# First loads of a DiT block: Wada's first half shared with ScalarE's queue, Wqkv's q and k in four pieces, the bias of the modulation added in four parts

## Chip, cores and metric

The kernel runs on one core of one Trainium2 chip. The metric is the device time of one execution in microseconds; several executions are given as a median with the lowest and the highest.

## What is computed

One transformer block with adaptive layer norm, in float32: x is 2 x 2048 x 512, 16 heads of 32, a hidden layer of 2048.

```python
mod = jax.nn.silu(condition) @ Wada + bada          # 2 x 3072
sh_a, sc_a, gt_a, sh_m, sc_m, gt_m = jnp.split(mod, 6, axis=1)
xn = _layernorm(x, g1, be1)
xm = xn * (1.0 + sc_a[:, None, :]) + sh_a[:, None, :]
x = x + gt_a[:, None, :] * _attention(xm, Wqkv, Wproj, bproj)   # causal
xn = _layernorm(x, g2, be2)
xm = xn * (1.0 + sc_m[:, None, :]) + sh_m[:, None, :]
h = jax.nn.gelu(xm @ W1 + b1, approximate=False)
x = x + gt_m[:, None, :] * (h @ W2 + b2)
```

## The kernel before

Batch row 0 is projected first (`Qkv`: four groups of 512 tokens), then its attention runs, then the same for batch row 1 with the output projection of row 0 ahead of it, and at last the two layers of the MLP for all tokens. The change touches only what stands ahead of and inside the first of these stages.

Ahead of the first group the kernel does this. Seven small DMAs on ScalarE's queue (line 1102) bring the condition and the columns of parameters (g1, be1, g2, be2, b1, b2) as rows of one tile, `rows`. SyncE's queue brings the four tiles of x of group 0 (`load_x`, line 796), then parts 0 and 1 of Wada (`load_wada`, line 1120: for each of the four chunks k of 128 rows, one DMA of 256 KB for either part), then Wqkv (`load_w`, line 803: q, k and v, 1 MB each), then the x of group 1. GpSimd brings bada into the tile `mr` (line 1114).

The computation around it, in the order in which each engine has it:

- PE: `ps_c` (line 212, the transpose of `rows`), eight transposes of the first two x tiles (`ps_xt`), the sixteen passes of `ps_mod` (the modulation, silu of the condition times Wada, line 1148), eight transposes of the other two x tiles, `ps_modt` (line 1158: `mr` to columns, four products of two passes each), then group 0's products: `ps_qk` (line 842; q and k blocks of 128 columns in turn) and `ps_v`.
- DVE: the statistics of the four x tiles (line 216), some constants, `cols` (line 1130, a copy of `ps_c`), the reciprocal of the standard deviations (line 223), the four normalized x tiles (line 241), then `mr` (line 1153, `ps_mod` plus bias), the columns a and c, and with ScalarE the modulated tokens `xmT`.
- ScalarE: its DMAs, a table load and a first square root, `rstd` (line 222), another table load, and the silu of the condition (`sc`, line 1184), which needs `cols`.

Nothing of x goes through `ps_mod`; the two meet in `xmT`. Still each engine works in order, and so `ps_xt` stands behind `ps_c`, `ps_mod` behind the first `ps_xt`, and the reciprocal behind `cols`.

The framework that schedules the kernel orders instructions on DVE, ScalarE, GpSimd and the queues by its own estimate; PE's order, and what is wrapped in `act`, is that of the program. It gives the DMAs issued by SyncE and ScalarE eight completion counters, one after the other in turn. A DMA that gets a counter again waits, before it is issued, until the DMA that had that counter eight DMAs earlier has landed. All that the queue holds behind it waits too. In the program before, the DMAs come in this order: cond, x0, g1, x1, be1, g2, x2, be2, x3, b1, b2, the eight of Wada, the three of Wqkv, the four of the next x. So x3 waits for cond, b1 for x0, b2 for g1, the first of Wada for x1.

Later in this stage `load_wada(2, 5)` is called in group 0 and `load_wada(3, 4)` in group 1, all on SyncE's queue; their modulations run in groups 1 and 2, between the products. `columns` adds the bias in each of the three calls; for parts 2 and 5 it then ends, since these are gates that are kept as rows.

Of the kernel before, what the change touches and what calls it, by code (L numbers as in the profile page):

```python
# [12 lines left out]
ALU = mybir.AluOpType  # L13
# [4 lines left out]
P = 128  # L18
# [9 lines left out]
def dit_block_kernel(  # L28
# [36 lines left out]
    nc = tc.nc  # L65
    B, T, D = x.shape
# [17 lines left out]
    def pool(name, bufs=1, **kw):  # L84
        return tc.tile_pool(name=name, bufs=bufs, reuse_waits="tile", **kw)
# [31 lines left out]
    for n in range(2):  # L117

        f = bp.tile([P, QB + P], BF16, tag=f"fold{n}", name=f"fold{n}")
# [10 lines left out]
    def picks():  # L130
        two = ident.rearrange("p (k r b) -> p k r b", k=2, r=2)[:, :, :, :B]
        nc.vector.tensor_tensor(pickc, two[:, 0], two[:, 1], ALU.add)
# [6 lines left out]
    cols = const.tile([P, 64], F32, tag="cols", name="cols")  # L139
# [55 lines left out]
    def col(r, n):  # L195
        return cols[:, r : r + n]
# [5 lines left out]
    def mm(*args, **kw):  # L202

        return tc.keep_in_program_order(nc.tensor.matmul(*args, **kw))  # L204

    def act(ins):

        return tc.keep_in_program_order(ins)

    def transpose(dst, src):  # L210
        n = src.shape[0]
        return tc.keep_in_program_order(nc.tensor.transpose(dst, src, ident[:n, :n]))  # L212
# [571 lines left out]
    class Qkv:  # L784
# [12 lines left out]
                xts.append(xt)  # L797
            self.xts[g] = xts

        def load_w(self, queue):  # L800
            w_v = Wqkv.rearrange("(c p) f -> p c f", p=P)
            for f in range(0, 3 * D, D):
                act(queue.dma_start(self.w[:, :, f : f + D], w_v[:, :, f : f + D]))

        def stats(self, g, t, keep=False):

# [282 lines left out]
    with pool("wada") as wp, pool("qkv0") as qp, pool(  # L1089
        "ps_qkv0", bufs=6, space=PSUM  # L1090
    ) as ps_mm:
        rows = wp.tile([n_rows, P], F32, tag="rows", name="rows")
        for r, n, src in (
            (0, n_cond, cond.rearrange("b (c p) -> (b c) p", p=P)),
            (r_g1, C, g1.rearrange("(c p) -> c p", p=P)),
            (r_be1, C, be1.rearrange("(c p) -> c p", p=P)),
            (r_g2, C, g2.rearrange("(c p) -> c p", p=P)),
            (r_be2, C, be2.rearrange("(c p) -> c p", p=P)),
            (r_b1, FC, b1.rearrange("(c p) -> c p", p=P)),
            (r_b2, C, b2.rearrange("(c p) -> c p", p=P)),  # L1100
        ):
            nc.scalar.dma_start(rows[r : r + n, :], src)
        wada_v = Wada.rearrange("(c p) f -> p c f", p=P)
        wada = {}

        def load_wada(s0, s1):
            w = wp.tile([P, 2, C, D], F32, tag="wada", name="wada")
            if s0 % 3 == 2:
                mr = modr
            else:  # L1110
                mr = wp.tile([P, D], F32, tag="mr", name="mr")
                nc.gpsimd.memset(mr, 0.0)
            for n, s in enumerate((s0, s1)):
                nc.gpsimd.dma_start(
                    mr[n * HD : n * HD + B, :],
                    bada[s * D : (s + 1) * D].partition_broadcast(B),
                )
            for k in range(C):
                for n, s in enumerate((s0, s1)):
                    nc.sync.dma_start(w[:, n, k, :], wada_v[:, k, s * D : (s + 1) * D])  # L1120
            wada[s0] = w, mr

        qkv = Qkv(row, qp, ps_mm)
        qkv.load_x(0)
        load_wada(0, 1)
        qkv.load_w(nc.sync)

        ps_c = ps_mm.tile([P, n_rows], F32, tag="mm", name="ps_c")
        transpose(ps_c, rows)
        nc.vector.tensor_copy(cols[:, :n_rows], ps_c)  # L1130
        sc = wp.tile([P, C, HD], F32, tag="sc", name="sc")
        nc.vector.memset(sc, 0.0)

        def modulation(s0):

            w, mr = wada.pop(s0)  # L1140
            ps = ps_sp.tile([P, D], F32, tag="s", name="ps_mod")
            for k in range(C // 2):
                for half in range(2):
                    for n in range(2):
                        at = (2 * half + n) * HD
                        kk = half * C // 2 + k
                        mm(
                            ps[at : at + HD, :], sc[:, kk, :], w[:, n, kk, :],
                            start=(k == 0), stop=(k == C // 2 - 1),
                        )  # L1150

            def columns():
                nc.vector.tensor_tensor(mr, ps, mr, ALU.add)
                if s0 % 3 == 2:
                    return
                ps_t = ps_sp.tile([P, C, 2, B], F32, tag="s", name="ps_modt")
                for k in range(C):
                    mm(
                        ps_t[:, k], mr[:, k * P : (k + 1) * P], pickc,
                        start=True, stop=True,  # L1160
                    )
                nc.vector.tensor_copy(
                    mod[:, s0 : s0 + 2], ps_t.rearrange("p c s b -> p s c b")
                )

            return columns

        def scale_shift(a, c, r_g, r_be, shift, scale):

            for dst, r in ((a, r_g), (c, r_be)):  # L1170
                nc.vector.scalar_tensor_tensor(
                    dst, mod[:, scale], 1.0,
                    col(r, C).unsqueeze(2).to_broadcast([P, C, B]),
                    ALU.add, ALU.mult,
                )
            nc.vector.tensor_tensor(c, c, mod[:, shift], ALU.add)

        for t in range(MTT):
            qkv.stats(0, t)
        qkv.normalize(0, 0)  # L1180
        halves = [qkv.norm(0, 0)]

        act(
            nc.scalar.activation(
                sc[:, :, :B], col(0, n_cond).rearrange("p (b c) -> p c b", c=C), AF.Silu
            )
        )
        picks()
        columns = modulation(0)
        qkv.normalize(0, 1)  # L1190
        halves.append(qkv.norm(0, 1))
        columns()
        scale_shift(a1, c1, r_g1, r_be1, 0, 1)
        for k in range(0, C, 2):
            for modulate in halves:
                modulate((k, k + 1))
        act(nc.vector.tensor_copy(pick, pickc.unsqueeze(3).to_broadcast([P, 2, B, P])))

        def also(g, n):

            if g == NG - 1 and n % 2 == 0:
                quarters.step()
            if g == 0 and n == 2:
                load_wada(2, 5)
            elif g in (1, 2) and n == 3:
                qkv.columns = modulation(g + 1)
            elif g in (1, 2) and n == 4:
                qkv.columns()
                if g == 1:
                    load_wada(3, 4)  # L1210
                else:
                    scale_shift(a2, c2, r_g2, r_be2, 3, 4)

        quarters = Quarters()
        with pool("hl0") as hp:

            def rooms():

                w = wp.tile([P, 2 * C * D], F32, tag="wada", name="w7")
                return [w[:, k * piece : (k + 1) * piece] for k in range(2)]  # L1220

            quarters.more_rooms = rooms
            qkv.run(hp, also)
            quarters.store()
# [5 lines left out]
    with pool("qkv1") as qp, pool("ps_qkv1", bufs=6, space=PSUM) as ps_mm:  # L1230
        qkv = Qkv(row, qp, ps_mm)
# [725 lines left out]
```

## Time and profile before

| | us |
|---|---|
| median of 3 executions | 2307.09 |
| lowest, highest | 2304.53, 2312.58 |
| the profiled execution | 2305.74 |
| its span, first to last instruction | 2304.0 |
| mean granted TensorE clock | 0.999 |
| PE busy in the span | 2257.0 |

The views used below are the page's busy shares, the busy time by stretches, the instructions in order of time, the waits, and the instructions of one tile. "PE" are TensorE's products, "PEld" its weight loads, "SPq", "ACTq" and "POOLq" the DMA issues of an engine. In the order of time a row gives start, duration, engine, line, operation, output and inputs, the count of merged instructions, and in brackets how long the engine was idle before and what ended that. In a stretch's row stand start and end, length, the busy time and count of each engine, the granted clock, the DMA engines' busy share and GB/s. Packets and sizes of DMAs are decimal in GB/s; a tile of 128 x 512 float32 is 256 KB.

### The profile page before, as it was taken

The numbers are of one execution on the slowest core, as the hardware profiler recorded it, in microseconds if no ns is written. First come the engines' busy times: TensorE is split into PE (matmuls) and PEld (weight loads), VectorE is DVE, ScalarE is ACT, GpSimd is POOL, SyncE is SP. The second block draws the span as 40 slices with busy tenths as digits, with TensorE's granted clock in tenths as the row PEclk, the third lists the DMA queues.
The fourth block names the chain that finished last, engine by engine and source line by source line (L and its number), as shares of the span: only waits on it lengthen the run. The fifth ranks groups of instructions, "written<-read, shape, count | busy, mean of one in ns | idle before, by whom it ended". The sixth has DMA issues, their size and how long they took to land. (4 is left out here: it accounts for less than half of the span.)

```text
span 2304.0 us, 33430 instructions
## 1 busy us (share of the span) xinstructions
PE 2257.0 (98%) x12141; PEld 1385.4 (60%) x12141; DVE 1544.9 (67%) x3089; ACT 940.6 (41%) x1780; POOL 1290.5 (56%) x1036
## 2 busy tenths in 40 slices
PE   8999999999999999999999999999999999999998
PEld 3455555555544445544555545446888888888887
DVE  3367776777766525667677777555896876877787
ACT  2222555555565122245555555632332242252230
POOL 1042987878793564468789787553664602602510
PEclk9999999999999999999999999999999999999999
DMA  7678206151233799971421504265375654654643
GB/s 256 201 224 208 63 24 136 31 120 47 59 130 117 245 303 308 322 231 29 93 69 34 116 24 131 87 226 197 119 272 202 210 177 160 201 181 151 213 145 116
DMA packets 118524, 355.60 MB, mean 154 GB/s; under 512 B 14496, under 2 KB 15052, under 8 KB 103640
## 3 DMA queue, kind: packets, MB, share of 16 engines
q1 hardware_dynamic: 107040, 293.64, 42.4%
q0 software_dynamic: 10944, 59.28, 7.2%
q8 instruction: 96, 1.57, 0.3%
q14 instruction: 68, 0.56, 0.1%
q10 hardware_dynamic: 376, 0.55, 0.1%
HBM read 253.80 MB, written 107.48 MB: 157 GB/s over the span
## 5 line engine op out<-in xcount | busy, mean ns | idle before, releaser
L608 ACT ACTIVATE e<-st 128x512 f32<-128x512 f32 (+1 forms) x1152 | 573.4, 579 | 403.2 <-PE st L204 358.0
L473 DVE TENSOR_REDUCE mx<-s 128x1 f32<-128x512 f32 x612 | 413.4, 687 | 193.3 <-PE s L204 192.0
L638 POOL TENSOR_TENSOR ee<-ee,e 128x1024 f32<-128x1024 f32 x212 | 498.6, 2385 | 7.6 <-ACT e L608 7.6
L204 PE MATMUL s<-kst,qst 128*128 128x512 f32 (+3 forms) x1032 | 472.7, 459 | 11.9 <-DVE mx L473 5.8
L204 PE MATMUL st<-qst,kst 128*128 128x512 f32 (+3 forms) x1280 | 400.9, 378 | 0.0
L204 PE MATMUL ps_a<-sum,room 128*128 128x256 f32 x1504 | 356.8, 381 | 4.7 <-DVE c L1440 1.7
L204 PEld LDWEIGHTS ps_a<-sum,room 128*128 128x128 f32 x1504 | 281.2, 190 | 54.5 <-issue 6.0
L204 PE MATMUL o<-e,vv 128*32 128x512 f32 (+3 forms) x2560 | 303.0, 539 | 5.1 <-POOL e L617 5.1
L468 DVE CUSTOM_DVE_ANT_0 junk<-s,causal 128x128 bf16<-128x128 f32 (+3 forms) x420 | 206.1, 491 | 124.2 <-PE s L204 116.7
L204 PEld LDWEIGHTS s<-kst,qst 128*128 128x128 f32 x1032 | 193.9, 188 | 143.4 <-issue 65.2
L204 PEld LDWEIGHTS st<-qst,kst 128*128 128x128 f32 x1280 | 229.0, 188 | 68.1 <-issue 38.9
L638 POOL TENSOR_TENSOR ee<-e 128x1024 f32<-128x1024 f32 x84 | 198.3, 2381 | 122.5 <-ACT e L608 114.9
L204 PE MATMUL ps_qk<-xmT,wqkv 128*128 128x512 f32 x512 | 239.0, 594 | 1.8 <-DVE xmT L275 1.8
L617 POOL TENSOR_SCALAR_AFFINE_SELECT e<-e 128x256 f32<-128x256 f32 x256 | 103.7, 438 | 94.4 <-ACT e L608 92.3
L204 PEld LDWEIGHTS ps_qk<-xmT,wqkv 128*128 128x128 f32 x512 | 93.9, 190 | 97.2 <-issue 90.5
L1668 POOL TENSOR_TENSOR c<-c,h 128x512 f32<-128x512 f32 x40 | 58.6, 1485 | 159.4 <-ACT c L1666 159.4
L204 PEld LDWEIGHTS <-sel 32*128 32x128 bf16 x1152 | 29.7, 91 | 192.4 <-issue 190.3
L204 PE MATMUL ps_b<-sum,room 128*128 128x256 f32 x608 | 143.6, 379 | 0.0
L204 PEld LDWEIGHTS o<-e,vv 128*32 128x32 f32 x2560 | 61.8, 108 | 104.3 <-issue 80.3
L204 PEld LDWEIGHTS ps_b<-sum,room 128*128 128x128 f32 x608 | 115.0, 190 | 15.4
L204 PE MATMUL ps_v<-wqkv,xmT 128*128 128x512 f32 x256 | 122.1, 594 | 0.0
L204 PE MATMUL st<-fold,sel 32*128 32x512 bf16 (+1 forms) x1152 | 117.6, 372 | 4.3 <-DVE mhl L494 2.8
(180 smaller groups left out, 2939.2 us busy)
## 6 DMA issues: line engine op xcount, KB each, us to landing
qst<-q SPq DMA_DIRECT2D x128, 256.0 KB
room<-w1e SPq DMA_DIRECT2D x28, 1024.0 KB
kst<-k SPq DMA_DIRECT2D x24, 1024.0 KB
room<-w1e SPq DMA_DIRECT2D x28, 768.0 KB
room<-w2e SPq DMA_DIRECT2D x21, 1024.0 KB
q<-hl SPq DMA_DIRECT2D x32, 512.0 KB
k<-hl SPq DMA_DIRECT2D x32, 512.0 KB
room<-w2e SPq DMA_DIRECT2D x21, 768.0 KB
```

Of the source, the lines that this page charges most:

```text
L204: return tc.keep_in_program_order(nc.tensor.matmul(*args, **kw))
L468: nc.vector.tensor_tensor_reduce(junk[:, :w], s[:, :w], causal[:, QB - w :], 1.0, MASKED, ALU.add, ALU.max, m,)
L473: nc.vector.tensor_reduce(m, s[:, :w], axis=AX.X, op=ALU.max)
L608: act(nc.scalar.activation(e[:, h % 2, :w], sts[h][:, :w], AF.Exp))
L617: nc.gpsimd.affine_select(d, d, pattern=[[0, 2], [1, P]], compare_op=ALU.is_ge, fill=0.0, base=0, channel_multiplier=-1,)
L638: act(engine.tensor_tensor(dst, x, y, ALU.add))
L1668: nc.gpsimd.tensor_tensor(c, c, piece_of(base, i, t, pair), ALU.add)
```

## The change

Chunks 0 and 2 of Wada's parts 0 and 1 are issued by ScalarE, chunks 1 and 3 by SyncE, each as one DMA of both parts (512 KB). ScalarE's rows are split: cond stays first, the six others are written in the program behind x and Wada. Wqkv's q and k come in halves of 256 columns, q, k, q, k, and then v whole. The bias is added in four parts of 128 columns, except for parts 2 and 5. `load_wada(3, 4)` has adjoining parts too and becomes four DMAs on SyncE; `load_wada(2, 5)` stays at eight.

```diff
-        def load_w(self, queue):
+        def load_w(self, queue, cols=range(0, 3 * D, D), n=D):
             w_v = Wqkv.rearrange("(c p) f -> p c f", p=P)
-            for f in range(0, 3 * D, D):
-                act(queue.dma_start(self.w[:, :, f : f + D], w_v[:, :, f : f + D]))
+            for f in cols:
+                act(queue.dma_start(self.w[:, :, f : f + n], w_v[:, :, f : f + n]))
...
-        for r, n, src in (
+        rows_of_cols = (
...
-        ):
-            nc.scalar.dma_start(rows[r : r + n, :], src)
+        )
+
+        def load_rows(some):
+            for r, n, src in some:
+                nc.scalar.dma_start(rows[r : r + n, :], src)
...
             for k in range(C):
+                queue = nc.scalar if s0 == 0 and k % 2 == 0 else nc.sync
+                if s1 == s0 + 1:
+                    queue.dma_start(
+                        w[:, :, k, :],
+                        wada_v[:, k, s0 * D : (s1 + 1) * D].rearrange(
+                            "p (n d) -> p n d", d=D
+                        ),
+                    )
+                    continue
                 for n, s in enumerate((s0, s1)):
                     nc.sync.dma_start(w[:, n, k, :], wada_v[:, k, s * D : (s + 1) * D])
             wada[s0] = w, mr
 
         qkv = Qkv(row, qp, ps_mm)
+        load_rows(rows_of_cols[:1])
         qkv.load_x(0)
         load_wada(0, 1)
-        qkv.load_w(nc.sync)
+        load_rows(rows_of_cols[1:])
+        half = D // 2
+        qkv.load_w(nc.sync, (0, D, half, D + half), half)
+        qkv.load_w(nc.sync, (2 * D,))
...
             def columns():
-                nc.vector.tensor_tensor(mr, ps, mr, ALU.add)
+                per = D if s0 % 3 == 2 else P
+                for k in range(0, D, per):
+                    part = mr[:, k : k + per]
+                    nc.vector.tensor_tensor(part, ps[:, k : k + per], part, ALU.add)
```

PE's instructions and their order are the same in both programs.

## The prediction

> **What bounds the kernel now.** I read the busy shares first, then PE by stage, then the first microseconds in order of time.
>
> ```profile
> PE 2257.0 (98%) x12141; PEld 1385.4 (60%) x12141; DVE 1544.9 (67%) x3089; ACT 940.6 (41%) x1780; POOL 1290.5 (56%) x1036
> ...
> 0.00:20.00 20.00, 9.40 (x44) 5.31 (x45) 10.05 (x35) 4.88 (x9) 6.31 (x20) 1.00 0.88 303
> 20.00:160.00 140.00, 139.36 (x419) 67.82 (x418) 62.30 (x167) 36.89 (x63) 21.48 (x30) 1.00 0.72 219
> ```
>
> PE is busy 98% of the span. Of its 47 us of idle time, 10.6 lie in the first 20 us, and only 0.64 in the next 140, in which batch row 0 is projected. The edits lie in those two stretches. So what moves is when the first `ps_qk` starts: from there PE runs without a gap, and what stands behind it in order moves by as much. This is the start in order of time (start, duration, instruction, idle before it and its releaser):
>
> ```profile
> 0.81 2.39 SPq L796 DMA_DIRECT2D x<-in_x_dram  x4
> 3.54 0.69 ACTq L1102 DMA_DIRECT2D rows<-in_L_cond_b_dram  x2
> 3.54 0.69 DVE L216 BATCH_NORM_STATS2 stat<-x 128x6 f32<-128x512 f32 x1 [2.17 <-DMA x<-in_x_dram]
> 4.26 1.28 ACT L136 ACT_TABLE_LOAD   x1 [4.26 <-DMA x<-in_x_dram]
> 4.43 3.81 SPq L1120 DMA_DIRECT2D wada<-in_L_cond_Wada_dram  x8
> 4.43 0.69 DVE L216 BATCH_NORM_STATS2 stat<-x 128x6 f32<-128x512 f32 x1
> 6.84 0.66 DVE L216 BATCH_NORM_STATS2 stat<-x 128x6 f32<-128x512 f32 x1
> 7.23 0.30 PE L212 MATMUL ps_c<-ident,rows 44*128 44x44 f32 x1 [7.23 <-DMA rows<-in_L_cond_b_dram]
> 7.75 0.30 ACT L222 ACTIVATE rstd<-mv,eps 128x4 f32<-128x4 f32 x1 [1.99 <-DVE mv L219]
> 8.00 0.15 DVE L115 COPY tmask<-tmask 128x1 f32<-128x1 f32 x1
> 8.06 0.20 DVE L1130 COPY cols<-ps_c 128x44 f32<-128x44 f32 x1
> 8.24 0.17 DVE L223 RECIPROCAL rstd<-rstd 128x4 f32<-128x4 f32 x1
> 8.28 2.48 SPq L803 DMA_DIRECT2D wqkv<-in_L_cond_Wqkv_dram  x3
> 9.12 2.21 PE L212 MATMUL ps_xt<-ident,x 128*128 128x128 f32 x8 [1.59 <-DVE x L241]
> 11.27 3.86 PE L204 MATMUL ps_mod<-wada,sc 128*32 128x512 f32 x16
> 12.11 0.18 PEld L204 LDWEIGHTS ps_mod<-wada,sc 128*32 128x32 f32 x2 [0.66 <-DMA wada<-in_L_cond_Wada_dram]
> 12.81 0.35 PEld L204 LDWEIGHTS ps_mod<-wada,sc 128*32 128x32 f32 x6 [0.51 <-DMA wada<-in_L_cond_Wada_dram]
> 13.45 0.37 PEld L204 LDWEIGHTS ps_mod<-wada,sc 128*32 128x32 f32 x2 [0.29 <-DMA wada<-in_L_cond_Wada_dram]
> 14.08 0.14 PEld L204 LDWEIGHTS ps_mod<-wada,sc 128*32 128x32 f32 x2 [0.27 <-DMA wada<-in_L_cond_Wada_dram]
> 15.06 0.86 PEld L212 LDWEIGHTS ps_xt<-ident,x 128*128 128x128 f32 x8 [0.84 <-issue]
> 15.22 0.69 DVE L1153 TENSOR_TENSOR mr<-ps_mod,mr 128x512 f32<-128x512 f32 x1 [4.78 <-issue]
> 15.97 0.97 PEld L204 LDWEIGHTS ps_modt<-pickc,mr 128*128 128x128 f32 x8
> 18.80 24.30 PE L204 MATMUL ps_qk<-xmT,wqkv 128*128 128x512 f32 x56 [1.78 <-DVE xmT L275]
> ```
>
> Two things must meet before `ps_mod`: Wada, and a chain from the rows of parameters: `ps_c`, `cols`, on DVE then the reciprocal and the normalized x, `ps_xt`, `ps_mod`. The rows end at 7.23, x at 6.84; Wada's waits then cost 0.66 + 0.51 + 0.29 + 0.27 = 1.73 us inside `ps_mod`, which is what the change can win.
>
> The rows also show how DMAs are issued. The eight completion counters of SyncE's and ScalarE's DMAs are used in turn, and a DMA is not issued before the one eight earlier has landed. ScalarE's b1 stood eight behind the first x and was issued at 3.54, when that landed; SyncE's first Wada stood eight behind the second x and went at 4.43, when that landed. SP's waits say the same:
>
> ```profile
> SPq L1120 <- DMA x<-in_x_dram: 1.5, 2, 1.2
> ```
>
> **Half of Wada on ScalarE: what it moves.** In the built program the DMAs now come in this order: cond, x0, Wada chunk 0 (ACT), x1, x2, Wada chunk 2 (ACT), x3, Wada chunk 1 (SP), g1, be1, g2, Wada chunk 3 (SP), be2, b1, b2, Wqkv. So eight back from g2 is Wada chunk 0, and eight back from b1 is Wada chunk 2: 512 KB pieces. b1 can't be issued before 1 MB of Wada has landed through ScalarE's queue. b2 stands behind it, then ACT's table load (1.28), a column of 0.2 and `rstd` (0.30), which so end at least 2.5 after b1's issue; the rows need longer, as follows. `ps_c` takes all the rows, is first on PE, and `cols` stands ahead of the reciprocal on DVE. The rows, off the critical side before, now end last.
>
> When does chunk 2 land? The first x has the DMA engines to itself; then ScalarE's 4 quarter megabytes share them with SyncE's x1 to x3 and half of chunk 1. If the queues take turns, chunk 2 is the ninth quarter megabyte. Before, the ninth (four x and five of Wada) was there at 12.11: that wait of `ps_mod` is for chunk 2, whose first piece was Wada's fifth. The bounds come from the rates:
>
> ```profile
> 2.00:14.00 12.00, 5.18 (x22) 2.67 (x23) 6.07 (x20) 3.28 (x5) 3.40 (x8) 1.00 0.92 304
> 14.00:22.00 8.00, 6.22 (x31) 3.48 (x27) 3.51 (x10) 1.93 (x4) 1.55 (x3) 1.00 1.05 393
> ```
>
> Nine quarters are 2.36 MB. At 393 GB/s from 2.0 on they end at 8.0; if ScalarE's queue comes last of all Wada, at 14.08. I take 12.1, the row that counts landings of the same pieces. [...]
>
> From b1's issue to `ps_c` it took 7.23 - 3.54 = 3.69 us, with x and Wada under way; the same pair goes out again beside Wada and Wqkv, so I take 3.69. The low bound is the first x on empty queues, 0.81 to 3.54: 2.73. From `ps_c` the reciprocal needs 0.30 + 0.06 (to `cols`) + 0.18 = 0.54; before it was 1.01, since DVE was busy to 8.06 with `tmask`. So the reciprocal comes at 12.1 + 3.69 + 0.54 = 16.33 instead of 8.24: 8.09 late, and with it `ps_xt` and `ps_mod`, which follow as before.
>
> **What is won.** By 19.4 (16.33 and the 3.03 from 8.24 to 11.27) all Wada has landed, so the 1.73 of waits go. Not all of that is gained, for TensorE was slow while they passed:
>
> ```profile
> L212 PE MATMUL ps_xt<-ident,x x8: 421/421/474, 9.1 to 10.9; 128*128 128x128 f32 x8
> L212 PE MATMUL ps_xt<-ident,x x8: 272/272/330, 15.1 to 15.9; 128*128 128x128 f32 x8
> L204 PE MATMUL ps_mod<-wada,sc x16: 592/892/1062, 11.3 to 14.5; 128*32 128x512 f32 x16
> ```
>
> The same transpose takes 421 ns at 9.1 us and 272 at 15.1, a `ps_mod` pass 1062 at first and 592 at last: twice the pace, from somewhere near four microseconds after the first `ps_xt`. `ps_mod`'s 16 passes lie in four column strips side by side, four deep. The fast pace is 24.30 / 56 = 0.43 a pass, the slow one twice that, 0.87. With two slow and two fast passes and 0.16 to drain it takes 2.76 instead of 3.86: 1.10 won. Bounds: all slow 0.2, all waits 1.73. [...]
>
> **Bias in four parts: nothing.** `ps_modt` can't start before the second `ps_xt` block leaves PE, 15.06 + 0.86 = 15.92, and the whole add ends at 15.22 + 0.69 = 15.91. Four adds of 128 columns cost between 0.20 each (`cols`' 44 columns) and 0.69 / 2 = 0.35: they end 0.8 to 1.4 after 15.22, and the last pair of `ps_modt` is only due at 15.97 + 0.73 = 16.70. If they took longer than 1.5, PE would wait for the rest. The later use (parts 3 and 4, in group 2) lies in the stretch where PE idles 0.64 in 140.
>
> **Wqkv in pieces, and SP's queue.** The first piece is issued when Wada chunk 1 has landed, later than 8.28. `ps_qk` would start at 18.80 + 6.99 = 25.8. From 14.1 the q and k pieces (2.1 MB) need 5.3 us at 393 GB/s and 6.9 at 304: they end by 21.0, V by 24.4, the next x by 27.9, for statistics first due at about 34. No row shows rows of 1 KB; were they half as fast as 304, the first two pieces would still be there at 21. Cost nothing either way; without the delay above, pieces in turn would let the first K block start half a megabyte sooner, which nobody waits for (the 1.78 before `ps_qk` is for xmT). Of Wada's parts 2 and 5, four pieces now stand ahead of the first q store on SP and the rest behind it; they are needed a group later. DVE and ACT change their order in group 0 to 2 a little; PE's cover there is the 0.64.
>
> **Sum.** +8.09 - 1.10 = +6.99, on the profiled execution's 2305.74 us (span 2304.0): **2312.7 us**. That run is 1.35 under the median shown, 2307.09, by which it would be 2314.1. A measurement of this kernel tells about 0.3% from no change, 6.9 us here: the forecast sits on that bound.
>
> **Rivals.** *Not slower: chunk 2 lands early.* If ScalarE's pieces get past x or the engines run at 393 from the start, chunk 2 lands at 8.0: 8.0 + 3.69 + 0.54 - 8.24 = 3.99, less 1.10: +2.9, 2308.6. With 2.73 for the rows and all 1.73 won it is +1.3, 2307.0. It decides below a landing of 12.0; for it speaks the mean rate of 304, by which nine quarters end at 9.8, against it that x's four (1.05 MB, 5.5 by that rate) landed only at 6.84. *Later still:* chunk 2 comes with the last of Wada, 14.08: 14.08 + 4.23 - 8.24 - 1.10 = +9.0, 2314.7; with 0.2 won, 2315.6. *The change does what it says:* the rows don't bind, Wada is early: -1.1 to -1.7, 2304.0 to 2304.6; within the bound too. For it: only if counters were not used in turn, which 3.54 and 4.43 contradict.
>
> **How the numbers follow.** Forecast with its own spread (landing 12 to 13.5) 0.42; later still 0.10; chunk 2 before 12.0 0.40; no delay 0.08. Slower by over 0.3%: 0.52. Within: 0.43, the early cases. Faster: 0.05, out of the last case and the runs' own spread (2304.53 to 2312.58), since 6.9 us are not to be had from 1.73. The range goes from the early case's low end, 2306.5, to the late one's high end on the median, 2317.5.
>
> **What would show it.** Right: `ps_c` ends its wait near 15.8 on a b row, ACT's b issues start near 12.1, `ps_mod` has no wait on Wada and takes about 2.8, `ps_qk` starts near 25.8, PE in 20 to 160 stays as full. Wrong: b issued before 9, or `ps_qk` before 20; a PE wait on Wqkv; a shift that is not the same at the start of attention and at the end.

## The result, and the profile after

Over 22 executions of each on the same chip the changed kernel takes 2311.01 us (2304.69 to 2315.15), the kernel before 2306.93 (2302.95 to 2312.78): ratio 1.0016, 95% interval 1.0009 to 1.0023. It is slower, by 3.7 us (0.0016 x 2306.93): within the 0.3% that the prediction called no change, though so many executions tell it apart from none. The medians themselves lie 4.08 apart. The profiled execution took 2309.83 us (span 2308.1), 4.09 more than before's.

The rows that answer to those of before are the busy shares and the stretches first:

```profile
PE 2258.2 (98%) x12141; PEld 1386.3 (60%) x12141; DVE 1547.9 (67%) x3095; ACT 941.0 (41%) x1780; POOL 1294.4 (56%) x1036
...
0.00:20.00 20.00, 6.87 (x30) 3.17 (x31) 7.36 (x29) 3.17 (x5) 4.76 (x17) 1.00 0.88 311
20.00:160.00 140.00, 137.59 (x412) 66.89 (x411) 61.26 (x167) 36.86 (x63) 18.19 (x26) 0.99 0.69 211
2.00:14.00 12.00, 0.87 (x3) 0.48 (x4) 5.48 (x19) 3.17 (x5) 3.40 (x8) 1.00 0.93 333
```

PE has 2.53 us less work in the first 20 us and 1.77 less in the next 140: 4.30 in all, the delay of the first `ps_qk`. The DMA engines moved 333 GB/s from 2 to 14 us where they had moved 304. The gain lies early, from 4 to 10 us (the first row is before's), and ends in a lull:

```profile
4.00:10.00 6.00, 1.18 (x4) 0.78 (x5) 5.16 (x20) 3.28 (x5) 1.40 (x3) 1.00 0.89 279
4.00:10.00 6.00, 0.00 (x0) 0.00 (x0) 3.12 (x10) 0.33 (x1) 1.40 (x3) 1.00 1.06 394
10.00:12.00 2.00, 0.00 (x0) 0.00 (x0) 0.42 (x5) 1.97 (x4) 0.00 (x0) 1.00 0.39 125
```

394 GB/s instead of 279: x and Wada had moved by 11.1, all but a hundredth of them by 10.5, where `ps_mod` had waited for Wada up to 14.08. Wada was thus there sooner, as the change wants; the rows now came last. Then the start of the changed kernel in order of time:

```profile
1.41 0.93 ACTq L1125 DMA_DIRECT2D wada<-in_L_cond_Wada_dram  x2
2.65 2.16 SPq L1125 DMA_DIRECT2D wada<-in_L_cond_Wada_dram  x2
3.60 0.69 DVE L216 BATCH_NORM_STATS2 stat<-x 128x6 f32<-128x512 f32 x1 [2.24 <-DMA x<-in_x_dram]
8.96 0.69 ACTq L1105 DMA_DIRECT2D rows<-in_L_cond_b_dram  x2
9.01 0.69 DVE L216 BATCH_NORM_STATS2 stat<-x 128x6 f32<-128x512 f32 x1 [1.27 <-DMA x<-in_x_dram]
12.09 0.30 PE L212 MATMUL ps_c<-ident,rows 44*128 44x44 f32 x1 [12.09 <-DMA rows<-in_L_cond_b_dram]
12.55 0.17 DVE L223 RECIPROCAL rstd<-rstd 128x4 f32<-128x4 f32 x1
13.43 2.21 PE L212 MATMUL ps_xt<-ident,x 128*128 128x128 f32 x8 [1.03 <-DVE x L241]
15.57 3.64 PE L204 MATMUL ps_mod<-wada,sc 128*32 128x512 f32 x16
19.14 1.37 PE L212 MATMUL ps_xt<-ident,x 128*128 128x128 f32 x8
19.34 0.88 DVE L1173 TENSOR_TENSOR mr<-ps_mod,mr 128x128 f32<-128x128 f32 x4 [4.59 <-issue]
20.36 0.95 PE L204 MATMUL ps_modt<-pickc,mr 128*128 128x4 f32 x8
23.09 5.40 PE L204 MATMUL ps_qk<-xmT,wqkv 128*128 128x512 f32 x8 [1.78 <-DVE xmT L275]
```

The mechanism is the predicted one. b1 and b2 are issued late, at 8.96, `ps_c` waits for them to 12.09, and the reciprocal, `ps_xt` and `ps_mod` follow. The reciprocal is 4.31 late (12.55 against 8.24), and `ps_qk` 4.29 (23.09 against 18.80). `ps_mod` no longer waits for Wada, but its passes all took the long time:

```profile
L204 PE MATMUL ps_mod<-wada,sc x16: 1061/1061/1062, 15.6 to 18.2; 128*32 128x512 f32 x16
```

So only 0.22 of its 3.86 went, not 1.10. And the first passes of `ps_qk` are long too; the granted clock stands third from the end of each stretch's row:

```profile
20.00:22.00 2.00, 1.31 (x13) 1.22 (x11) 0.80 (x6) 0.00 (x0) 0.53 (x1) 1.00 1.01 340
22.00:24.00 2.00, 0.92 (x1) 0.44 (x2) 1.97 (x5) 1.32 (x3) 1.03 (x2) 0.80 0.94 329
24.00:26.00 2.00, 2.00 (x4) 0.93 (x3) 0.27 (x1) 0.61 (x2) 0.00 (x0) 0.50 0.95 333
26.00:28.00 2.00, 2.00 (x5) 0.77 (x5) 0.00 (x0) 0.00 (x0) 0.00 (x0) 0.85 0.29 107
```

Half clock for 0.8 + 2.0 + 0.6 = 3.4 us costs 1.7. In the kernel before, the same stretch of `ps_qk` has a clock of 1.00:

```profile
20.00:22.00 2.00, 2.00 (x6) 0.85 (x5) 0.00 (x0) 0.32 (x1) 0.00 (x0) 1.00 1.05 382
```

Instruction by instruction against before, PE is 4.28 late at the first `ps_qk`, 5.98 after its long passes, and still 5.8 at 400 us. It is 2.4 late at 1001, because before loses 1.3 more in a wait between 980 and 1000 us and 1.7 in a window of half clock there, while the changed kernel has its own only after 1030. At the end it is 4.17. The last figure is thus 4.3 of delay, and windows of half clock that fall here in the one execution and there in the other. Over many executions the windows do not make the difference: the mean granted clock of the changed kernel's 22 is 0.9984, that of the kernel before 0.9984 to 0.9987 in the four groups below. Times 2305 us that is 3.8 us lost against 3.1 to 3.7.

### The profile page after: what moved, and what is told of

It is laid out like the page before. It is cut to its first block, busy times and chain, and to the rows that moved or that the text cites. A ratio compares the mean times of both kernels' runs of the same rounds, so it can differ in the third digit from the quotient of the medians.

```text
span 2308.1 us, 33431 instructions
## 1 busy us (share of the span) xinstructions
PE 2258.2 (98%) x12141; PEld 1386.3 (60%) x12141; DVE 1547.9 (67%) x3095; ACT 941.0 (41%) x1780; POOL 1294.4 (56%) x1036
```

## Experiments

All were run in five rounds beside the kernel before, in four groups on four chips (2305.25, 2304.53, 2305.83 and 2306.59 are the medians of before in them), so that ratios compare across groups and times do not. PE's delay in a profile is that of one execution; the ratio is of the medians.

**The Wada part alone.** The kernel before with only this part of the diff: chunks 0 and 2 on ScalarE's queue, adjoining parts as one DMA, six rows behind them.

```diff
+                queue = nc.scalar if s0 == 0 and k % 2 == 0 else nc.sync
...
+        load_rows(rows_of_cols[:1])
         qkv.load_x(0)
         load_wada(0, 1)
+        load_rows(rows_of_cols[1:])
```

> Before plus Wada's split alone (half of its first chunks on ScalarE, 512 KB each, six of the seven rows behind it); Wqkv stays in three pieces, the bias in one add. Theory: the whole cost is this part, through the counter that b1 shares with Wada's chunk 2: b1 issued near 9, ps_c near 12.1, ps_qk from 23.1, time +2.5 to +5 us on the kernel before. Rival: the pieces of Wqkv or the four adds carry part of it: then less than +2.

2310.45 us against 2305.25, ratio 1.0020 (1.0011 to 1.0029).

```profile
8.99 0.69 ACTq L1105 DMA_DIRECT2D rows<-in_L_cond_b_dram  x2
12.02 0.30 PE L212 MATMUL ps_c<-ident,rows 44*128 44x44 f32 x1 [12.02 <-DMA rows<-in_L_cond_b_dram]
15.50 2.43 PE L204 MATMUL ps_mod<-wada,sc 128*32 128x512 f32 x16
21.64 2.84 PE L204 MATMUL ps_qk<-xmT,wqkv 128*128 128x512 f32 x6 [1.78 <-DVE xmT L275]
```

The b rows, `ps_c` and `ps_mod`'s start are those of the whole change to 0.1 us: this part carries all of the cost in time (1.0020 against the whole change's 1.0016). Here TensorE turned fast inside `ps_mod`, so that 1.43 was won (3.86 - 2.43) and `ps_qk` is 2.84 late. Its profiled execution was the shortest of its eleven, 2305.54; the median is what counts.

**The other two parts alone.** The kernel before with Wqkv in pieces and the bias in four parts.

```diff
-        qkv.load_w(nc.sync)
+        qkv.load_w(nc.sync, (0, D, half, D + half), half)
+        qkv.load_w(nc.sync, (2 * D,))
```

> The other two parts alone: Wqkv's q and k in four pieces and the bias in four adds, Wada as before. Theory: nothing, within 1 us of the kernel before; ps_c at 7.2, ps_modt still not before the second ps_xt block leaves PE, ps_qk at 18.8 plus or minus 0.2, no PE wait on Wqkv. Rival: rows of 1 KB are slow and the next x or Wqkv is late, or four adds end later than ps_modt needs them: +1 to +3 us, with a wait in ps_modt or ps_qk.

2306.76 against 2305.25, ratio 1.0001 (0.9991 to 1.0011): nothing that can be told apart, as predicted. `ps_qk` starts 0.16 later and no instruction of PE waits for Wqkv.

```profile
18.96 5.21 PE L204 MATMUL ps_qk<-xmT,wqkv 128*128 128x512 f32 x8 [1.78 <-DVE xmT L275]
...
20.00:22.00 2.00, 2.00 (x4) 0.96 (x3) 0.14 (x1) 0.48 (x2) 0.00 (x0) 0.50 1.05 384
```

The window of half clock in `ps_qk` is here too, without a late row: it does not come from the late rows.

**All rows first.** The changed kernel, with the seven rows ahead of x and Wada again.

```diff
-        load_rows(rows_of_cols[:1])
+        load_rows(rows_of_cols)
         qkv.load_x(0)
         load_wada(0, 1)
-        load_rows(rows_of_cols[1:])
```

> The changed kernel with all seven rows of parameters issued ahead of x and Wada on ScalarE's queue, so that no row takes over a counter from Wada. Theory (counters): b1 issued near 3.5, ps_c at 7.2 to 7.5; ScalarE's table load waits for the issue of chunk 2 (behind the third x), so rstd some 0.5 later than before; ps_xt near 9.6, ps_qk 18.5 to 19.5, time within 1 us of the kernel before. Rival (sharing): the second queue by itself makes x late, the fourth x at 9.0 instead of 6.8 as in the changed kernel: then ps_xt not before 11, ps_qk from 20.5, time +2 us.

2308.32 against 2305.25, ratio 1.0013 (1.0003 to 1.0023).

```profile
3.56 0.69 ACTq L1105 DMA_DIRECT2D rows<-in_L_cond_b_dram  x2
4.43 1.15 ACTq L1125 DMA_DIRECT2D wada<-in_L_cond_Wada_dram  x2
13.20 0.20 PEld L204 LDWEIGHTS ps_mod<-wada,sc 128*32 128x32 f32 x8 [2.14 <-DMA wada<-in_L_cond_Wada_dram]
19.62 4.56 PE L204 MATMUL ps_qk<-xmT,wqkv 128*128 128x512 f32 x10 [1.78 <-DVE xmT L275]
```

The late rows are cured (b at 3.56, `ps_xt` at 8.73), but now `ps_mod` begins at 10.87 and, after the passes of its first chunk, waits 2.14 for the next, which by its order is chunk 2 of ScalarE's queue, and `ps_qk` is still 0.82 late. Neither theory had this whole. Wada was issued only from 4.2 on, and its next chunk was waited for to 13.20, where the changed kernel had all of Wada by 11.1: the second queue alone does not bring it sooner. The time is another matter: `ps_qk` comes 3.5 us earlier than in the changed kernel, and the ratio falls only from 1.0016 to 1.0013, well inside the intervals. That the late rows make the loss in time is thus read from the changed kernel's profile; this run does not confirm it.

**One queue, in order of use.** The same, and Wada's four 512 KB chunks all on SyncE in the order in which `ps_mod` takes them.

```diff
-            for k in range(C):
-                queue = nc.scalar if s0 == 0 and k % 2 == 0 else nc.sync
+            for k in (0, 2, 1, 3):
+                queue = nc.sync
```

> All seven rows first, and Wada's four chunks of 512 KB all on SyncE's queue in the order in which ps_mod reads them (0, 2, 1, 3); Wqkv in pieces and the bias in four parts stay. Against the run with the rows first, in which chunk 2 came from ScalarE and ps_mod stood 2.14 us for it. Theory (two queues that take turns bring all chunks in at the end, one queue brings them in order): no PE wait over 0.8 on Wada, ps_qk at 18.2 to 19.0, time within 1 us of the kernel before and 1 to 2 less than with the rows first. Rival (512 KB pieces land late on any queue): a wait of 1.5 or more stays.

2305.38 against 2304.53, ratio 1.0004 (0.9995 to 1.0012).

```profile
17.77 10.61 PE L204 MATMUL ps_qk<-xmT,wqkv 128*128 128x512 f32 x17 [1.78 <-DVE xmT L275]
...
18.00:20.00 2.00, 2.00 (x3) 0.94 (x4) 0.95 (x3) 1.29 (x3) 0.00 (x0) 0.50 1.05 384
20.00:22.00 2.00, 2.00 (x3) 0.67 (x2) 0.00 (x0) 0.00 (x0) 0.00 (x0) 0.50 1.07 384
```

`ps_qk` starts 1.03 earlier than before, and 1.85 earlier than with two queues: here the loads do gain. Whether the one queue or the order of use does it was not separated, and the ratio is no clear gain on 1.0013. In the profile two windows of half clock, from 17.1 to 23.9, give back 3.0.

**b1 and b2 issued by GpSimd.** The changed kernel, with only these two rows taken off ScalarE's queue.

```diff
-                nc.scalar.dma_start(rows[r : r + n, :], src)
+                queue = nc.gpsimd if r in (r_b1, r_b2) else nc.scalar
+                queue.dma_start(rows[r : r + n, :], src)
```

> The changed kernel with the b1 and b2 rows issued by GpSimd, whose queue has counters of its own; cond and the other four rows stay on ScalarE behind Wada's two chunks. It splits the delay of the rows: the counter of b1 (nothing is issued before chunk 2 has landed at 9.0) against standing in ScalarE's queue behind 1 MB. Theory (counter): be2 goes out near 7.3 as before, so the rows are complete near 9.5 to 10.3 instead of 12.1, ps_c then; 2 us less than the changed kernel, +1 to +3 on the kernel before. Rival (the queue): rows behind 1 MB of Wada land no sooner than 11.5 to 12, and nothing is won.

2310.28 against 2304.53, ratio 1.0028 (1.0018 to 1.0038).

```profile
7.67 0.26 ACTq L1106 DMA_DIRECT2D rows<-in_L_cond_be_dram  x1
12.38 0.30 PE L212 MATMUL ps_c<-ident,rows 44*128 44x44 f32 x1 [12.38 <-DMA rows<-in_L_cond_be_dram]
```

be2 is issued at 7.67, 1.3 earlier than b1 was, and `ps_c` still waits for it to 12.38: 4.7 us for 2 KB, where the b rows took 3.1 and 3.7 from issue to `ps_c`. The counter of b1 was thus not the only hold (be2 itself follows g2, which goes out only at 7.32). be2 stands in ScalarE's queue behind 1 MB of Wada, and the 12.38 lies near the 11.5 to 12 of the rival that puts the delay there; that its place in the queue is the cause was not isolated. Open too is the time: `ps_qk` starts at 20.66, 2.4 earlier than in the changed kernel, with no window of half clock in this stage, and the median is still 5.75 above before.

**Products ahead of `ps_c`.** The changed kernel, with 36 products of the identity with itself (72 passes) on PE while it waits for the rows. Nobody reads their results.

```diff
+        for _ in range(4):
+            ps_w = ps_mm.tile([P, 512], F32, tag="mm", name="ps_warm")
+            for k in range(9):
+                mm(ps_w[:, :P], ident, ident, start=True, stop=True)
         transpose(ps_c, rows)
```

> The changed kernel with 36 products of the identity (72 passes) ahead of ps_c, whose result nobody reads; they fill PE's idle time while the rows are awaited, to about 11.5. Theory (the pace of TensorE follows its own activity): ps_c still near 12.1, the first ps_xt block in 1.3 or less instead of 2.2, ps_mod in about 1.9 instead of 3.6, ps_qk near 20.3 and no slow passes in it, so 3 to 4.5 us less than the changed kernel: within 1 us of the kernel before. Rival (the slow passes belong to what they read, tiles just landed by DMA): ps_mod keeps 3.6 and the time stays that of the changed kernel.

2303.74 against 2305.25, ratio 0.9994 (0.9984 to 1.0005).

```profile
12.91 1.44 PE L212 MATMUL ps_xt<-ident,x 128*128 128x128 f32 x8 [0.24 <-DVE x L241]
14.63 1.92 PE L204 MATMUL ps_mod<-wada,sc 128*32 128x512 f32 x16 [0.28 <-ACT sc L1208]
20.19 4.10 PE L204 MATMUL ps_qk<-xmT,wqkv 128*128 128x512 f32 x9 [1.82 <-issue]
```

With PE busy beforehand, `ps_mod` takes 1.92, a little over half of 3.64: it is the pace and not Wada that held it. `ps_qk` is 1.36 late instead of 4.29. That is 2.9 better. The rest of the profile's gain (it ends 4.1 ahead of the kernel before) comes between 997 and 1031 us, where this execution has neither a window of half clock nor the 3 us of idle time that before has from 1000 to 1040.

**The same on the kernel before**, with 16 products (32 passes):

```diff
+        for _ in range(2):
+            ps_w = ps_mm.tile([P, 512], F32, tag="mm", name="ps_warm")
+            for k in range(8):
+                mm(ps_w[:, :P], ident, ident, start=True, stop=True)
         transpose(ps_c, rows)
```

> The kernel before with 16 products of the identity (32 passes) on PE ahead of ps_c, to about 7.0. Theory (activity): the first ps_xt block takes 1.5 instead of 2.2, ps_mod's passes are fast, but its end is set by the landing of the last Wada piece near 14, so ps_qk comes 0.2 to 0.6 earlier at most; what else is won is that no execution has slow passes in ps_qk: -0.5 to -2 us in the median. Rival (no slow passes in most executions of the kernel before): within 0.5 us.

2307.0 against 2304.53, ratio 1.0008 (0.9999 to 1.0017): a miss. `ps_mod` then only waits for Wada (waits of 0.81, 0.56, 0.49 and 0.51), `ps_qk` starts 0.69 earlier, and a window of half clock at 19.0 to 22.4 takes 1.7.

**Everything together**: rows first, one queue in order of use, 16 products ahead of `ps_c`, and the second `ps_xt` block ahead of `ps_mod`. Beside the edits shown:

```diff
-        columns = modulation(0)
         qkv.normalize(0, 1)
         halves.append(qkv.norm(0, 1))
-        columns()
+        modulation(0)()
```

> A version from what was seen: all seven rows first, Wada's chunks on SyncE in the order of use, Wqkv in pieces, the bias in four adds, PE kept busy by 16 products ahead of ps_c, and the second ps_xt block ahead of ps_mod, so that ps_modt stands directly behind ps_mod and can start after the first of the four adds. Theory: ps_mod ends 0.3 to 0.8 after the last chunk, ps_modt starts 0.4 after ps_mod, ps_qk at 17.2 to 18.0 against 18.8, time -1 to -3 us on the kernel before (0.05% to 0.13%). Rival (the last landing of Wada and the slow runs of the rest hide it): within 0.5 us.

2309.31 against 2304.53, ratio 1.0023 (1.0013 to 1.0032): a miss, slower than before.

```profile
13.70 0.14 PEld L204 LDWEIGHTS ps_mod<-wada,sc 128*32 128x32 f32 x4 [1.33 <-DMA wada<-in_L_cond_Wada_dram]
15.20 1.05 PE L204 MATMUL ps_modt<-pickc,mr 128*128 128x4 f32 x8 [0.45 <-DVE mr L1176]
18.08 6.22 PE L204 MATMUL ps_qk<-xmT,wqkv 128*128 128x512 f32 x10 [1.82 <-issue]
```

Wada's end sets `ps_mod`, so a faster PE gains only waits (1.33 in the row, and 1.06 ahead of it). `ps_qk` is 0.72 early, and 0.95 late after a window of half clock at 18.2 to 21.6; at the end PE is 3.5 late. The median is 4.8 above before. Half of that is the clock: the mean of its ten executions is 0.9976, that of before's thirty 0.9987, 5.5 us lost against 3.1. The other half is not settled.

**Products in the gap ahead of `ps_qk`.** By then the windows in `ps_qk` had shown in five of the ten profiles (the changed kernel, the pieces alone, one queue, and the last two), and all ten have the 1.78 us (1.77 to 1.83) in which PE waits for `xmT`, right behind `ps_modt`'s small products. In the profiles of the changed kernel and of the kernel before, each change of the granted clock lies a whole number of 3.413 us after the first turn to the fast pace: the turn at 19.77 and the changes at 23.18, 26.60, 1030.12, 1033.53 and 2306.70 (1, 2, 296, 297 and 670 times) in the one, the turn at 13.58 and the changes at 996.61, 1000.03 and 2303.92 (288, 289 and 671 times) in the other. These are the stretches, so counted, around the gap, two of the changed kernel and one of the kernel before:

```profile
19.77:23.18 3.41, 1.63 (x16) 1.55 (x14) 2.17 (x10) 0.50 (x2) 1.52 (x3) 1.00 1.02 358
23.18:26.60 3.42, 3.42 (x5) 1.35 (x6) 1.09 (x3) 1.43 (x4) 0.04 (x1) 0.50 0.88 303
16.99:20.40 3.41, 1.63 (x5) 0.86 (x5) 2.81 (x9) 1.93 (x4) 1.55 (x3) 1.00 1.05 386
```

PE is busy for 1.63 in the first and in the third, but in the changed kernel most of that is `ps_modt` (0.95), and the stretch behind it runs at half clock; before, it is `ps_qk`, and nothing falls. Counted without `ps_modt`, PE's share of the 3.41 us ahead of the fall is 0.02 to 0.44 in the five profiles, and 0.47 in before's stretch. (In the run with one queue PE's share of the first 3.41 us at half clock is 0.81, and the clock stays down for as long again; in the four others it is 0.90 to 1.00, and the clock comes back.) In these profiles the falls in `ps_qk` thus stand behind a low share of products. That the share decides is not shown: at 996.61 us before's clock falls behind a stretch with 0.69 (2.36 of 3.41).

Six identity products cover the gap. The first kernel is that with one queue in order of use:

```diff
         columns()
+        ps_w = ps_mm.tile([P, 512], F32, tag="mm", name="ps_warm")
+        for k in range(6):
+            mm(ps_w[:, :P], ident, ident, start=True, stop=True)
         scale_shift(a1, c1, r_g1, r_be1, 0, 1)
```

> The kernel with the rows first and Wada's four 512 KB chunks on one queue in order of use, plus six products of the identity with itself (12 passes of 128 columns) behind ps_modt, in the 1.78 us in which PE waits for xmT. Theory: that idle stretch is what lets the granted clock fall inside ps_qk (0.5 for up to 3.41 us a window), so covered it does not fall there: the first ps_qk starts near 17.8 as in the run with one queue, no window below 0.8 between 18 and 30, and the time is 1 to 3 us under the kernel before. Rival 1: the windows come from the small products of ps_modt and ps_mod's waits for Wada, not from the idle 1.78: the clock still falls in ps_qk, and the time is that of the run with one queue, +0.5 to +1. Rival 2: the fillers run slow (12 passes of 0.21 us, 2.6) and push ps_qk later by 0.8: +1 to +2.

2303.40 against 2305.83, ratio 0.9985 (0.9976 to 0.9994).

```profile
16.12 1.58 PE L204 MATMUL ps_warm<-ident 128*128 128x128 f32 x12
18.04 8.42 PE L204 MATMUL ps_qk<-xmT,wqkv 128*128 128x512 f32 x19 [0.34 <-DVE xmT L275]
...
18.00:20.00 2.00, 1.96 (x5) 1.00 (x6) 1.22 (x3) 1.56 (x4) 0.17 (x1) 1.00 1.05 381
20.00:22.00 2.00, 2.00 (x6) 0.81 (x5) 0.00 (x0) 0.22 (x1) 0.00 (x0) 1.00 1.06 384
```

The window is gone, `ps_qk` is 0.76 early to the end of the stage, and this version beats both kernels. Against its parent, one queue without the products, the ratios to before are 0.9985 and 1.0004. With the 16 products ahead of `ps_c` as well:

> As the kernel with six identity products in the idle stretch ahead of ps_qk, and sixteen more (32 passes) ahead of ps_c. Theory: TensorE is at the fast pace from the first ps_xt on and stays there; ps_mod then waits for Wada's last chunk, and ps_qk starts at 17.0 to 17.8, with no clock below 0.8 up to 30: 1 to 4 us under the kernel before. Rival: the clock falls all the same in one window between 15 and 25, because ps_mod's waits (about 2 us in all) are an idle stretch of their own: +0 to +2, as the kernel before with the warm products alone.

2304.33 against 2305.83, ratio 0.9995 (0.9986 to 1.0004). `ps_qk` starts at 17.80, 1.00 early, and the clock stays at 1.00 up to 28 us, as the theory said; the time, 1.5 under before, is at the weak end of what it expected, and the extra products bring nothing measurable. Then the same six products on the changed kernel and on the kernel before, without another edit:

> The changed kernel plus six identity products (12 passes) behind ps_modt, in the 1.78 us in which PE waits for xmT. Theory: the part of the change's cost that the late rows make (ps_qk +4.3) stays, the part that the fallen clock makes inside ps_qk (+1.7 in the profiled run) goes: ps_qk starts at 23.1 to 23.5, no clock below 0.8 from 23 to 34, and the time is +2.0 to +3.0 on the kernel before, 1 to 2 us under the changed kernel's +3.7. Rival: that window had nothing to do with the idle stretch; the clock falls in ps_qk all the same and the time is +3.7 or, with fillers at the slow pace, +4.5.

> The kernel before with the six identity products in the idle stretch alone. If the gain of the run with one queue and these products (ratio 0.9985) came from rows first and one queue (-0.8 at ps_qk) and the covered stretch together, this one shows the stretch's share: 0 to -2 us, ratio 0.9990 to 1.0000, with ps_qk at 18.8. Rival: the stretch is all of it, -3 us or more, 0.9985. Other rival: before has no fallen clock in ps_qk to be saved, so nothing, or +0.5 for fillers that run slow.

2308.09 and 2303.92 against 2306.59: ratios 1.0006 (0.9995 to 1.0016) and 0.9988 (0.9979 to 0.9997).

```profile
23.02 7.56 PE L204 MATMUL ps_qk<-xmT,wqkv 128*128 128x512 f32 x17 [0.34 <-DVE xmT L275]
...
24.00:26.00 2.00, 2.00 (x6) 0.94 (x5) 0.21 (x1) 0.55 (x2) 0.00 (x0) 1.00 0.94 319
```

```profile
11.11 5.01 PE L204 MATMUL ps_mod<-wada,sc 128*32 128x512 f32 x16
19.79 10.57 PE L204 MATMUL ps_qk<-xmT,wqkv 128*128 128x512 f32 x24 [0.34 <-DVE xmT L275]
```

On the changed kernel (the first two rows) `ps_qk` is 4.22 late and stays at 4.22: no half clock. The time is +1.5 on before, under the 2 to 3 expected. On the kernel before, the six products are worth 2.7, nearer to the rival's 3 than to the 0 to 2 of the first theory: they do nearly all that the version with one queue does (0.9988 and 0.9985, well inside the intervals). Its profile does not show the gain: `ps_mod` stayed at the low pace to its end (1.05 from its last weight load, at 15.07, to the end at 16.12, as long as a slow pass), and `ps_qk` is 0.99 late. None of the four kernels with the gap covered shows a window in `ps_qk`; there PE is idle for 0.33 to 0.34 ahead of it. In three pairs with and without the products (the changed kernel, the kernel before, one queue) the ratio falls by 0.0010, 0.0012 and 0.0019, 2.3 to 4.4 us. A window of 1.7 in half of the executions would be 0.85. The clock of all executions shows more: its mean rises from 0.9984 to 0.9994, from 0.9984 to 0.9990 and from 0.9985 to 0.9991, which is 2.4, 1.4 and 1.5 us less lost. That is the whole gain on the changed kernel and a third to a half of it on the other two; the rest has no place yet, and where in the kernel the clock was won is known only for the profiled executions.

One more thing scatters single profiles. In both of the last profiles PE waits once, in the MLP, for one `c` (this row is of the kernel before with products):

```profile
2177.95 3.64 PE L204 MATMUL ps_a<-sum,room 128*128 128x256 f32 x8 [2.35 <-DVE c L1443]
```

The kernel with 32 passes ahead of before's `ps_c` has a like idle of 2.2 more at the same place, the one with one queue near 1822, the others none. It comes 1800 us and more behind the edits, in kernels with different ones, and its cause was not looked for.

## Why the prediction was right, and where not

The measured 2311.01 lies 1.7 under the forecast 2312.7 and inside its range. But the forecast had slower by over 0.3% as the likeliest case (0.52), and what came is the rival "chunk 2 lands early" (0.40), by the prediction's own sign: b issued before 9, at 8.96. By that rival 8.96 gives 8.96 + 3.69 + 0.54 - 8.24 - 1.10 = +3.85. The number came near by luck: the forecast delay of 6.99 was 2.9 more than the 4.08 between the medians, and 1.2 of that went since the forecast was counted from one execution, 2305.74, that lay 1.2 under the median of the 22. On the median shown it would have been 2314.1, 3.1 too much. One of its signs of being wrong came true as well: the shift is not the same everywhere, 5.98 at 25 us, 2.4 at 1001 and 4.17 at the end. And the range's ends, 2306.5 and 2317.5, lie 0.5 outside the cases that they are taken from (2307.0, and 2315.6 with 1.35 more).

| step | predicted | measured |
|---|---|---|
| chunk 2 has landed, b issued | 12.1 | 8.96 |
| b to `ps_c` | 3.69 | 3.13 |
| `ps_c` to the reciprocal | 0.54 | 0.46 |
| reciprocal late by | 8.09 | 4.31 |
| won in `ps_mod` | 1.10 | 0.22 |
| second `ps_xt` block, then `ps_modt` to `ps_qk` | as before | +0.28, -0.08 |
| `ps_qk` late by | 6.99 | 4.29 |
| half clock in `ps_qk` | none | +1.70 in this execution |

**Right: the chain.** Rows late, `ps_c`, reciprocal, `ps_xt`, `ps_mod`, `ps_qk`, then a PE without slack, in the profiles. The Wada part alone gives the whole of the cost, the other two parts nothing (1.0001), and no PE instruction waits for Wqkv. The last step, from `ps_qk` to the time, holds for the changed kernel (4.29, and 4.08 in the medians) but is no rule: over the kernels with an edit, the shift of the median and that of the first `ps_qk` in the one profile differ by -3.7 (the kernel before with the gap covered) to +5.5 us (everything together).

**Mis-sized: chunk 2's landing, and the step behind it.** The prediction took the landing before, 12.1, where the DMA engines moved 304 GB/s at a share of 0.92 from 2 to 14 us, and no higher rate. It was higher: 372 GB/s from 2.00 to 8.96, where before had 285. The rival's condition that the engines run at 393 nearly came true, and 8.96 lies between its 8.0 and the 9.8 of nine quarters at the mean rate. Wada's own end, 14.08 before, came at about 11. Why the rate was higher was not isolated: in the changed kernel the first Wada goes out at 1.41, before at 4.43, and in pieces of 512 KB. With two queues but Wada issued from 4.2 on a chunk was waited for to 13.20, so that the second queue as such is not shown to win any. That both queues move side by side, as the count of nine quarters has it, was right: by 8.06 ScalarE's had moved its 1.05 MB and SyncE's 1.22. And the landing before counted more than nine quarters: at 292 GB/s from 2.00 on, 2.95 MB had moved by 12.11, 11.3 quarters. There the landing of a piece was no measure of the bytes ahead of it.

**Incomplete: what holds the rows.** b1 went at 8.96, as a wait for chunk 2's counter has it, but with b1 and b2 elsewhere the rows are as late (`ps_c` at 12.38 for be2), and what holds be2 was not isolated. Undoing the hold on b1 alone did not undo the cost. The last x tile was late as well (9.01 instead of 6.84), which the prediction did not say; it stayed off the critical side.

**Mis-sized: the gain in `ps_mod`.** I took two slow and two fast passes, an estimate from the turn some four microseconds after the first `ps_xt` in before's trace. All were slow, the bound of 0.2; in the run with the Wada part alone the turn fell inside and 1.43 was won. The turn's time is not a constant behind the first `ps_xt`: it came at 13.6 before and only at 19.8 in the changed kernel, 4.5 and 6.3 after. What sets it was not shown.

**Not counted: the clock falls again ahead of `ps_qk`.** The prediction's rows had the 1.78 before `ps_qk`, and put no price on it. In five of ten profiles a window of half clock began inside that idle stretch, which stands behind about 1 us of 4-column products, or within 1 us after it; in the four with the stretch cut to 0.33 to 0.34 none did. In the difference of the medians this term is small, 0.1 to 0.7 us by the mean clocks, since the kernel before loses nearly as much to its own windows.

**Bias in four parts, pieces, SP's queue:** nothing, as forecast. Only where the second `ps_xt` block had been moved ahead of `ps_mod` did `ps_modt` stand behind the bias (0.45 of wait, and begun 0.35 after the adds' start at 14.85). A whole add takes 0.69, so there the four parts should help; no run of that order with one add was made.

## What to carry to other kernels

Small transfers that start a chain go ahead of the large ones in their queue: behind 1 MB of Wada, 2 KB issued at 7.67 were there at 12.4; with all rows ahead of the loads they were there at 7.32 and 6.75. The second queue was not shown to bring a load sooner: issued at 1.41, ahead of x's last tile, Wada had moved by 11.1, but with two queues and a start at 4.2 a chunk was waited for up to 13.20, and one queue in order of use then began `ps_qk` 1.85 earlier. Before working on loads, look for the short stretches in which TensorE stands still ahead of a dense stage: six products that nobody reads were worth as much (0.9988) as anything done to the loads.

## What the hardware showed

- The half-clock windows of the first stage lasted 3.4 us (23.18 to 26.60 in the changed kernel), with one queue two in a row (17.1 to 23.9), and one costs 1.7 where PE is dense. It shows in the granted clock (0.50), while the equally slow passes at the start (1061 ns in `ps_mod`) stand beside a clock of 1.00 in the same column: there the tile's durations have to be read.
- With Wqkv in halves (rows of 1 KB) the DMA engines moved 351 to 358 GB/s from 14 to 18 us in six profiles, with whole parts (rows of 2 KB) 399 to 401 in three. That the length of the rows is the cause was not isolated. Nothing waited for Wqkv, so the time does not show it.
- Executions of one program differ by over 10 us (2304.69 to 2315.15), more than the change moves. Profiles alone could not have decided: the Wada part's showed no loss at the end (0.2 before the kernel before), and its median is 5.2 above.
